# A last convolution by seven quarter products, group-norm sums on another engine, key products by chunk

## The chip, the core and the metric

The kernel runs on one core of a Trainium2 chip. The core has five engines with a queue each: TensorE (PE) multiplies matrices into PSUM, VectorE (DVE) and ScalarE (ACT) work elementwise and reduce, GpSimd (POOL) does a few elementwise operations, SyncE (SP) issues nearly all DMAs. Each engine works through its own instructions in order and waits on semaphores for the others. The metric is the time in microseconds of one execution; less is better.

## The reference

The input is 8 images of 512 channels of 32 x 32, in float32. Each goes through two layers with a residual each, `x = x + layer(group_norm(x))`, with group norms of 32 groups of 16 channels.

```
layer one:
  t  = silu(bn(conv1x1(gn(x), 512 -> 512)));  ys = [t[:256], t[256:]]
  twice (modules l = 0, 1):
      z = silu(bn(conv3x3(ys[-1], 256 -> 256)))
      q, k, v = conv1x1(z);  a = softmax(q . (k + rw + rh) / 8)   4 heads of 64
      ys.append(ys[-1] + silu(bn(conv1x1(a . v))))
  x = x + silu(bn(conv1x1(concat(ys), 1024 -> 512)))          the last convolution, "cv2"
layer two:
  h = relu(bn(depthwise3x3(gn(x))));  h = 0 where the channel's max |h| < 4
  h = relu(bn(conv1x1(h, 512 -> 512)));  h = 0 where the channel's max |h| < 0.001
  x = x + h
```

## The kernel before, in words

One loop over the 8 images (`for b in range(B)`, L958) issues all instructions. A small wrapper (`InOrder`, L33) keeps PE, DVE, ACT and SP in exactly the order in which the Python code issues them; the profile therefore shows L43 for nearly every instruction, and groups are told apart by tile names. Work of neighbouring images is interleaved by hand: lists of small pieces (`taps`, `stats`, `early`, `late`, `before`, `halves`, `finishes`) are emptied piece by piece with `pump(list, n)` between other work. So a piece's place in the code is its place in the engine queues.

An image passes these stages:

- cv1 (L520), the first 1x1 convolution, on 128 x 128 blocks of weights and 512 columns of the image: output chunks m = 2, 3 (tiles `ps_cv`, written to `yp[0]`) and then 0, 1 in halves (`ps_y`, to `y0`).
- conv3 (L559), the 3x3 convolution in a transformed domain: DVE makes six planes from `yp` in `vtmp`, `v` and the buffers `kr`, `vt`, `qy`, TensorE multiplies them (`ps_c`), DVE transforms back (`mid`, `sd`, `y`), ACT writes `z` by Silu.
- qkv (L707): key products for chunks 2 and 3 of the weights into two PSUM tiles `ps_qk`, each evicted by DVE into `kr` with the column term `rw` added (L736) and then given the row term by POOL (L737); value products `ps_v`, which reuse the same PSUM tiles; query products. Pieces of the list `bg` are pumped between them in the numbers `counts`.
- attention (L758): 32 steps of scores (`ps_s`), exponential on ACT (`e`), products with the values two steps later (`ps_av`), and a running sum of the exponentials on DVE (`sum`). At step 19 and after the last step, the sums over partitions are formed on TensorE (`ps_dn`), inverted on DVE and spread by two DMAs; z is scaled by them. Other work is pumped in at the steps in `QUIET` (L956). After the last step, `tail` issues TensorE work that covers the last inversion.
- cv2m (L880), the 1x1 convolution after the attention (`ps_m`), with its residual on DVE into `yp[1]` or `qy`.
- After the second module, cv2 (L898): for each of four output chunks m, eight input blocks k (`y0`, `yp[0]`, `yp[1]`, `qy`, two chunks each) times two halves n of 512 columns, 64 matmuls into a two-bank PSUM tile `ps_cv2`; ACT applies Silu over 1024 columns, DVE adds to `xt`. The weights come as four tiles of 512 KB in a ring of four SBUF buffers (`ring_sources`, L303), which also carries the other weights. A released buffer is refilled by the next DMA of the list.
- Layer two's front (L400): `group_norm` on `xt` in two groups of two chunks. For each chunk DVE makes `bn_stats` and `bn_aggr` (L366), then a small matmul with `g_sb` averages over the group (`pm`), DVE forms the deviations, a second small matmul (`pv`), POOL takes the power -1/2, ACT normalises into `xn` and multiplies by the middle tap into `ht`. Eight `taps` per chunk follow on DVE, Relu on ACT, and `prune` (L428): DVE's maximum, a comparison, and POOL's product with it. These taps lie in the cv2 stage and in the next image's cv1, qkv(0) and first attention.
- Layer two's back (L454): products `ps_pw`, in the next image's first module.

The last image has no successor; its layer two follows at once (L1089 to L1159), chunk by chunk. There `prune` uses `reaches` (L345), ACT's masked sum with a DVE comparison, and scales `wpw_sb` instead of `ht`. Image 0 has a cv2 of its own order, with parts of it begun beside its attention (`partial`), and it prepares the transformed weights of conv3.

PSUM has two two-bank tiles (`big`, for ps_s, ps_qk, ps_v, ps_c, ps_cv2), three single banks (`acc`, for ps_av, ps_m2, ps_y0, ps_pw) and one bank `mm` (pm, pv, ps_dn). SBUF has a pool of 11 work tiles of 128 x 1024.

Of the kernel before, what the change touches and what calls it, by code (L numbers as in the profile page):

```python
# [10 lines left out]
F32 = mybir.dt.float32  # L11
# [4 lines left out]
P = 128  # L16
# [47 lines left out]
def fast_kernel(  # L64
# [53 lines left out]
    def load(dst, b):  # L118
# [24 lines left out]
    u_dram = [  # L143
        [dram.tile([P, 2, 4, 2, P], F32, tag=f"u{l}_{i}", name=f"u{l}") for i in range(6)]
        for l in range(2)
    ]

    raw = [[t.rearrange("p a b -> p (a b)")[:, : 6 * C2] for t in (qy, kr, vt)]]
# [55 lines left out]
    def flat(ps):  # L204
        return ps.rearrange("p n f -> p (n f)")
# [5 lines left out]
    def phases(ap):  # L211

        return ap.rearrange("p (r h t) -> p r h t", h=F, t=F // 4)
# [10 lines left out]
    def pump(bg, n=1):  # L224

        for _ in range(min(n, len(bg))):
            piece = bg.pop(0)
            if piece is None:
                return
            piece()  # L230
# [72 lines left out]
    def ring_sources():  # L303
        for b in range(B):
            for l in range(2):
                for i in range(6):
                    yield u_dram[l][i].rearrange("p a b c d -> p (a b c d)"), 2048
                yield wqkv[:, l].rearrange("p k o -> p (k o)"), 1536
                if b == l == 0:
                    for m in range(2):  # L310
                        yield w2[:, :, m * P : (m + 1) * P], 1024
            for m in range(KC):
                yield w2[:, :, m * P : (m + 1) * P], 1024

# [32 lines left out]
    def reaches(t, i):  # L347


        keep = small.tile([P, 1], F32, tag="keep3", name="keep3")  # L350
        nc.scalar.activation(
            work_tile("over"), t, AF.Relu, bias=below[:, i : i + 1], accum_out=keep
        )
        nc.vector.tensor_scalar(keep, keep, 0.0, None, ALU.is_gt)
        return keep

    def group_norm(src, dst, chunks):

# [41 lines left out]
    def layer1_front(groups):  # L400

        norm = {}

        def normed(c):
            norm[c] = work_tile("xn")
            return norm[c]

        gn = [group_norm(xt, normed, chunks) for chunks in groups]  # L410

        def before(c):
            size = len(groups[0])
            gn[c // size][size + 2 + c % size]()
            nc.scalar.mul(ht[c], norm[c], dw[:, c, 4:5])

        def tap(c, t):
            dst, src = img(ht[c]), img(norm[c])
            dy, dx = t // 3 - 1, t % 3 - 1
            o = dst[:, max(0, -dy) : F - max(0, dy), max(0, -dx) : F - max(0, dx)]  # L420
            i = src[:, max(0, dy) : F - max(0, -dy), max(0, dx) : F - max(0, -dx)]
            nc.vector.scalar_tensor_tensor(o, i, dw[:, c, t : t + 1], o, ALU.mult, ALU.add)

        def relu(c):
            norm.pop(c)
            act(ht[c], ht[c], AF.Relu, BN4 + c)

        def prune(c):  # L428
            keep = small.tile([P, 1], F32, tag="keep", name="keep")
            nc.vector.tensor_reduce(keep, ht[c], AX.X, ALU.max)  # L430
            nc.vector.tensor_scalar(keep, keep, 4.0, None, ALU.is_ge)
            nc.gpsimd.tensor_scalar(ht[c], ht[c], keep, 1.0, ALU.mult, ALU.mult)

        if len(groups) == KC:

            def prune(c):

                keep = reaches(ht[c], 0)
                w = wpw_sb[:, c, :]
                nc.vector.tensor_scalar(w, w, keep, None, ALU.mult)  # L440

            return [list(g) for g in gn], before, tap, relu, prune
        taps = []
        for c in range(KC):
            mine = [lambda c=c, t=t: tap(c, t) for t in range(9) if t != 4]
            if c:

                mine[2] = lambda c=c, t=mine[2]: (t(), relu(c - 1))
                mine[5] = lambda c=c, t=mine[5]: (t(), prune(c - 1))
            taps += mine  # L450
        taps += [lambda: relu(KC - 1), lambda: prune(KC - 1)]
        return gn[0][:4], gn[1][:4], [lambda c=c: before(c) for c in range(KC)], taps

# [253 lines left out]
    def qkv(l, bg, counts):  # L707
        counts = list(counts)
        with Weights() as wt:
            w = wt[:, : 6 * C2].rearrange("p (k o) -> p k o", k=2)  # L710

            def products(ms):

                tiles = [big_tile("ps_qk") for _ in ms]
                for k in range(2):
                    for m, ps in zip(ms, tiles):
                        for n in range(2):
                            nc.tensor.matmul(
                                ps[:, n, :],
                                w[:, k, m * P : (m + 1) * P],  # L720
                                z[:, k, n * 512 : (n + 1) * 512],
                                start=(k == 0),
                                stop=(k == 1),
                            )
                return tiles

            pump(bg, counts.pop(0))
            for m, ps in enumerate(products((2, 3))):
                kk = phases(kr[:, m, :])
                full = [P, 4, F, F // 4]  # L730
                col = rw[:, l, m, :].rearrange("p (t r) -> p r t", r=4)
                row = rh[:, l, m, :].unsqueeze(1).unsqueeze(3)

                col = col.unsqueeze(2).to_broadcast(full)
                for r in (slice(0, 2), slice(2, 4)):
                    nc.vector.tensor_tensor(kk[:, r], phases(flat(ps))[:, r], col[:, r], ALU.add)  # L736
                nc.gpsimd.tensor_tensor(kk, kk, row.to_broadcast(full), ALU.add)  # L737
                pump(bg, counts.pop(0))
            for g in range(2):
                ps = ps_big.tile([P, 4, C2], F32, tag="big", name="ps_v")  # L740
                for j in range(4):
                    jt = 4 * g + j
                    for k in range(2):
                        nc.tensor.matmul(
                            ps[:, j, :],
                            z[:, k, jt * P : (jt + 1) * P],
                            w[:, k, 2 * C2 : 3 * C2],
                            start=(k == 0),
                            stop=(k == 1),
                        )  # L750
                nc.scalar.copy(vt[:, 4 * g : 4 * g + 4, :], ps)
                pump(bg, counts.pop(0))
            for m in range(2):
                (ps,) = products((m,))
                nc.scalar.copy(qy[:, m, :], flat(ps))
                pump(bg, counts.pop(0))
# [123 lines left out]
    def cv2m(l):  # L880
        for n in range(2):
            for m in range(2):
                ps = bank_tile("ps_m2")
                for k in range(2):
                    nc.tensor.matmul(
                        ps,
                        wm2_sb[:, l, k, m * P : (m + 1) * P],
                        z[:, k, n * 512 : (n + 1) * 512],
                        start=(k == 0),
                        stop=(k == 1),  # L890
                    )
                t = work_tile("m2")[:, :512]
                act(t, ps, AF.Silu, BN3 + 2 * l + m)
                r = slice(2 * n, 2 * n + 2)
                dst = inner(yp[1], m) if l == 0 else phases(qy[:, m, :])
                nc.vector.tensor_tensor(dst[:, r], phases(t), inner(yp[l], m)[:, r], ALU.add)

    def cv2():  # L898
# [53 lines left out]

        return products, finish, partial


    QUIET = (5, 8, 11, 14, 17, 18, 24, 26, 27, 28, 29, 30)  # L956
    halves, finishes, taps, before, late = [], [], [], [], []
    for b in range(B):  # L958
        if b:
# [1 line left out]
            pump(first)  # L961
            pump(taps, 2)
            pump(first)
            pump(taps, 2)
            pump(first)
            pump(late)
            pump(taps, 2)
            pump(first)
            pump(late)
            pump(taps)  # L970
            pump(before, 2)
            pump(y0_work, 2)
            conv3(0, y0_work, 1, [])
            if b + 1 < B:
# [55 lines left out]
        load(xt, b)  # L1030
        stats = group_norm(pt, lambda c: pt[c], range(KC)) if b + 1 < B else []
        qkv(1, [], (0,) * 7)
        if b:
            products, finish, _ = cv2()

        def beside():
            products(0, range(6) if b else (4, 5))
            if b == 0:
                products(1, (3, 4, 5))

        attention(stats[:KC], (6, 10, 14, 17), beside)
        stats = stats[KC:]
        cv2m(1)
        if b == B - 1:
            break
        early, late, before, taps = layer1_front(((0, 1), (2, 3)))
        if b:
            products(1, (0, 1, 2, 3))
        pump(stats)
        if b:  # L1050
            products(1, (4, 5))
        products(0, (6, 7))
        pump(stats)
        finish(0)
# [45 lines left out]
    pump(gn[0])  # L1100
    products(1, (2, 3, 4))
    pump(gn[0])
    products(1, (5,))
    pump(gn[0])
    before(0)
    products(1, (6, 7))
    taps(1)
    finish(1)
    pump(gn[1])
# [505 lines left out]
```

## Time and profile before

| | us |
|---|---|
| median of 4 runs (2679.45 to 2680.41) | 2680.34 |
| the profiled execution, as timed | 2679.96 |
| its span, from the first to the last instruction | 2678.2 |
| granted TensorE clock, mean over the span | 0.997 |
| one middle image, from cv2 to cv2 | 327.4 |
| DVE busy in one middle image | 239 |
| ACT busy in one middle image | 140 |

The page counts the busy time of each engine, follows the chain of work that ended last, and lists the costliest groups of instructions. A float32 matmul leaves two records in the profile. The windows give the busy time of each engine in a stretch of the span, and the timeline lists instructions in order of time with the idle time before them in brackets and what ended it. The middle images repeat each other to within 0.3 us.

### The profile page before, as it was taken

The numbers are of one execution on the slowest core, as the hardware profiler recorded it, in microseconds if no ns is written. First come the engines' busy times: TensorE is split into PE (matmuls) and PEld (weight loads), VectorE is DVE, ScalarE is ACT, GpSimd is POOL, SyncE is SP. The second block draws the span as 40 slices with busy tenths as digits, with TensorE's granted clock in tenths as the row PEclk, the third lists the DMA queues.
The fourth block names the chain that finished last, engine by engine and source line by source line (L and its number), as shares of the span: only waits on it lengthen the run. The fifth ranks groups of instructions, "written<-read, shape, count | busy, mean of one in ns | idle before, by whom it ended". The sixth has DMA issues, their size and how long they took to land.

```text
span 2678.2 us, 36189 instructions
## 1 busy us (share of the span) xinstructions
PE 2627.2 (98%) x14958; PEld 1414.2 (53%) x14958; DVE 1955.9 (73%) x2692; ACT 1152.5 (43%) x1417; POOL 162.5 (6%) x99
## 2 busy tenths in 40 slices
PE   7999999999999999999999999999999999999997
PEld 5364464644646446464465545655455654646443
DVE  8886598774986759766697667976578865888557
ACT  3535436252352534535345343444335343353533
POOL 1000010000100001000010000100001000010000
PEclk9999999999999999999999999999999999999998
DMA  8441231302303013030130302312122221303100
GB/s 329 150 151 43 71 130 32 130 20 69 138 25 130 17 63 138 25 130 17 63 138 27 128 17 78 123 60 95 32 91 95 75 79 48 106 32 99 56 16 33
DMA packets 89340, 220.78 MB, mean 82 GB/s; under 512 B 5840, under 2 KB 53200, under 8 KB 76624
## 3 DMA queue, kind: packets, MB, share of 16 engines
q1 hardware_dynamic: 85616, 214.98, 23.5%
q10 hardware_dynamic: 3552, 3.41, 0.4%
q8 instruction: 119, 1.95, 0.3%
q14 instruction: 53, 0.43, 0.1%
HBM read 172.23 MB, written 29.36 MB: 75 GB/s over the span
## 4 chain that ended last, share of the span: by engine, by line
PE 90%; DVE 5%; ACT 1%; DMA 1%; issue 1%; POOL 0%; SPq 0%; POOLq 0%; ACTq 0%; DVEq 0%
PE ps_cv L43 19%; PE ps_av L43 16%; PE ps_s L43 16%; PE ps_c L43 11%; PE ps_pw L43 7%; PE ps_qk L43 7%; PE ps_v L43 4%; PE ps_m L43 4%; PE ps_y L43 4%; DVE kr L43 1%; PE ps_dn L43 1%; DVE ht L43 1%; ACT qy L43 1%; DMA u<-ucomp 1%; DVE mid L43 0%
## 5 line engine op out<-in xcount | busy, mean ns | idle before, releaser
L43 ACT ACTIVATE e<-ps_s 128x1024 f32<-128x1024 f32 x512 | 524.2, 1024 | 281.0 <-PE ps_s L43 271.5
L43 PE MATMUL ps_s<-qy,kr 64*64 64x512 f32 x4096 | 571.7, 592 | 1.7 <-ACT e L43 0.2
L43 PE MATMUL ps_av<-e,vt 64*64 64x512 f32 x4096 | 570.9, 591 | 1.6 <-ACT part L43 1.6
L43 DVE TENSOR_TENSOR sum<-sum,e 128x1024 f32<-128x1024 f32 x384 | 471.3, 1227 | 83.1 <-ACT e L43 76.9
L43 DVE SCALAR_TENSOR_TENSOR ht<-xn,v_sb,ht 128x961 f32<-128x961 f32 (+1 forms) x256 | 336.0, 1318 | 25.0 <-ACT ht L43 19.9
L43 PEld LDWEIGHTS ps_av<-e,vt 64*64 64x64 f32 x4096 | 219.3, 133 | 232.2 <-issue 155.6
L43 PEld LDWEIGHTS ps_s<-qy,kr 64*64 64x64 f32 x4096 | 203.8, 133 | 250.8 <-issue 139.7
L43 PE MATMUL ps_pw<-ht,wpw_sb 128*128 128x512 f32 x512 | 226.7, 598 | 7.2 <-DVE wpw_sb L43 7.1
L43 PE MATMUL ps_cv<-yp,wring 128*128 128x512 f32 x512 | 231.0, 599 | 0.0
L43 PE MATMUL ps_qk<-z,wring 128*128 128x512 f32 x512 | 225.7, 593 | 3.3 <-ACT z L43 3.3
L43 DVE TENSOR_TENSOR sum<-e 128x1024 f32<-128x1024 f32 x64 | 78.4, 1224 | 174.7 <-ACT e L43 173.7
L43 PEld LDWEIGHTS ps_pw<-ht,wpw_sb 128*128 128x128 f32 x512 | 96.4, 191 | 129.7 <-issue 120.3
L43 PEld LDWEIGHTS ps_qk<-z,wring 128*128 128x128 f32 x512 | 96.8, 190 | 119.2 <-issue 110.8
L43 PEld LDWEIGHTS ps_cv<-yp,wring 128*128 128x128 f32 x512 | 96.4, 191 | 115.2 <-issue 114.4
L737 POOL TENSOR_TENSOR kr<-kr,v_sb 128x1024 f32<-128x1024 f32 x32 | 69.7, 2186 | 1042.1 <-DVE kr L43 1042.1
L43 ACT COPY c<-ps_c 128x256 f32<-128x256 f32 x96 | 35.5, 369 | 208.6 <-PE ps_c L43 202.4
L43 PE MATMUL ps_v<-wring,z 128*128 128x256 f32 x512 | 114.3, 381 | 8.2 <-DVE kr L43 8.2
L43 PEld LDWEIGHTS ps_c<-kr,wring 128*128 128x128 f32 x1024 | 116.8, 192 | 10.4 <-issue 6.0
L43 DVE RECIPROCAL r<-ps_dn 128x128 f32<-128x128 f32 x128 | 114.7, 927 | 6.9 <-ACT r L43 6.9
L43 PE MATMUL ps_c<-kr,wring 128*128 128x128 f32 x1024 | 117.3, 275 | 2.3 <-ACT kr L43 2.3
L43 PE MATMUL ps_c<-vt,wring 128*128 128x128 f32 x1024 | 117.3, 275 | 1.6 <-DMA wring<-u 0.9
L43 PE MATMUL ps_c<-qy,wring 128*128 128x128 f32 x1024 | 117.7, 276 | 0.2 <-issue 0.2
(138 smaller groups left out, 2982.4 us busy)
## 6 DMA issues: line engine op xcount, KB each, us to landing
wring<-u SPq DMA_DIRECT2D x96, 1024.0 KB, 4.8
wring<-in_w SPq DMA_DIRECT2D x34, 512.0 KB, 4.3
pt<-in_x SPq DMA_DIRECT2D x32, 512.0 KB, 5.9
rw<-r SPq DMA_DIRECT2D x64, 256.0 KB, 3.4
xt<-in_x SPq DMA_DIRECT2D x32, 512.0 KB, 6.0
out<-xt SPq DMA_DIRECT2D x32, 512.0 KB, 2.9
wring<-in_wqkv SPq DMA_DIRECT2D x16, 768.0 KB, 4.3
u<-ucomp SPq DMA_DIRECT2D x24, 256.0 KB, 3.4
```

The source lines that it names most:

```text
L43: made = method(*args, **kwargs)
L737: nc.gpsimd.tensor_tensor(kk, kk, row.to_broadcast(full), ALU.add)
```

## The change

Three things change, and the schedule of the pumped pieces with them.

1. For images 1 to 6, cv2 is computed by seven products of quarters (Strassen's scheme in Winograd's form): weights and inputs are seen as 2 x 2 blocks (256 outputs by 512 inputs, 512 inputs by 512 columns). Four combinations of the weights, s1 to s4, and copies of a11, a12 and a22 are made once in image 0, during its second attention, and stored in DRAM; the ring brings them as two tiles of 1536 and two of 2048 columns instead of four of 1024. Four combinations of the inputs, t1 to t4, are made by DVE in every such image (in `kr`, `z`, `vt` and two work tiles), and the outputs are put together from the products by DVE additions. Silu then works on halves of 512 columns. Images 0 and 7 keep the eight products.
2. Layer two's group norm, in all images, takes its sums on ACT: a Copy with accumulated output, then, after the mean, a Square with the mean as bias and accumulated output. In images 0 to 6 `prune` of chunks 0 and 1 uses `reaches` in place of DVE's maximum.
3. The key products of qkv run chunk by chunk instead of input block by input block (except in image 0), and the two half additions of the column term become one.

```diff
+    QUARTERS = (("a11", "s1", "a12"), ("s2", "s3", "a22", "s4"))
+    s_dram = [ [ dram.tile([P, len(q), 4, P], F32, ...) for i, q in enumerate(QUARTERS) ] for p in range(2) ]
...
+            if 0 < b < B - 1:
+                for i in range(2):
+                    for p in range(2):
+                        yield s_dram[p][i].rearrange("p q k o -> p (q k o)"), 512 * (3 + i)
+                continue
             for m in range(KC):
                 yield w2[:, :, m * P : (m + 1) * P], 1024
...
+    def group_norm_scalar(src, dst, chunks):
...
+        def over(i, c, func, o, **bias):
+            nc.scalar.activation(ht[c], src[c], func, accum_out=o[:, i : i + 1], **bias)
+        def means():
+            nc.tensor.matmul(pm[:, :n], g_sb, sums, start=True, stop=True)
+            nc.vector.tensor_scalar(gm, pm[:, :n], -1.0 / HW, None, ALU.mult)
+            for i, c in enumerate(chunks):
+                over(i, c, AF.Square, sq, bias=gm[:, i : i + 1])
+        def deviations():
+            nc.tensor.matmul(pv[:, :n], g_sb, sq, start=True, stop=True)
+            nc.vector.tensor_scalar(rs, pv[:, :n], 1.0 / HW, 1e-5, ALU.mult, ALU.add)
+            nc.gpsimd.tensor_tensor(rs, rs, mhalf[:, :n], ALU.pow)
...
+        work = [lambda i=i, c=c: over(i, c, AF.Copy, sums) for i, c in enumerate(chunks)]
...
-        gn = [group_norm(xt, normed, chunks) for chunks in groups]
+        gn = [group_norm_scalar(xt, normed, chunks) for chunks in groups]
...
         def prune(c):
+            if c < 2:
+                keep = reaches(ht[c], 0)
+            else:
                 keep = small.tile([P, 1], F32, tag="keep", name="keep")
                 nc.vector.tensor_reduce(keep, ht[c], AX.X, ALU.max)
...
-                for k in range(2):
-                    for m, ps in zip(ms, tiles):
+                order = [(k, i) for i in range(len(ms)) for k in range(2)]
+                for k, i in sorted(order) if by_input else order:
...
-            for m, ps in enumerate(products((2, 3))):
+            for m, ps in enumerate(products((2, 3), b == 0)):
...
-                for r in (slice(0, 2), slice(2, 4)):
-                    nc.vector.tensor_tensor(kk[:, r], phases(flat(ps))[:, r], col[:, r], ALU.add)
+                nc.vector.tensor_tensor(
+                    kk, phases(flat(ps)), col.unsqueeze(2).to_broadcast(full), ALU.add
+                )
...
+    def combine_weights(p):
+...
+    def quartered():
+        rights = {
+            "a11": b11, "s1": t1, "a12": b21, "s2": t2, "s3": t3, "a22": t4, "s4": b22,
+        }
+        def product(p, name, cs=range(4)):
...
+                nc.tensor.matmul(
+                    banks[p, name],
+                    w[:, QUARTERS[i].index(name), c, :],
+                    rights[name][c],
+                    start=(c == 0),
+                    stop=(c == 3),
+                )
...
+        def keep_first():
...
+                nc.scalar.copy(kept[p, "m1"], banks[p, "a11"])
...
+        def plus(p, o, x, name):
...
+            nc.vector.tensor_tensor(kept[p, o], kept[p, x], banks[p, name], ALU.add)
...
+        def finish(p, low, n, x, name):
...
+            nc.vector.tensor_tensor(t, kept[p, x], banks[p, name], ALU.add)
+            act(t, t, AF.Silu, BN1 + m)
...
             pump(first)
             pump(taps, 2)
             pump(first)
-            pump(taps, 2)
-            pump(first)
             pump(late)
             pump(taps, 2)
             pump(first)
             pump(late)
-            pump(taps)
-            pump(before, 2)
+            pump(taps, min(3, len(taps) - 19))
+            pump(before)
+            pump(first)
+            pump(taps, min(2, len(taps) - 18))
+            pump(before)
             pump(y0_work, 2)
...
+            def beside():
+                for p in range(2):
+                    product(p, "a11")
+                keep_first()
+                right(0, range(4))
+                for p in range(2):
+                    product(p, "a12", (0, 1))
...
+        attention(work, (2, 4, 6, 8, 10, 11, 12, 14, 16, 18) if b == 0 else (6, 10, 14, 17), beside)
...
         if b:
-            products(1, (0, 1, 2, 3))
+            right(1, (0, 1))
+            product(0, "s1")
+            right(1, (2, 3))
+            product(0, "a12", (2, 3))
+            product(1, "a12", (2, 3))
+            finish(0, 0, 0, "m1", "a12")
+            right(2, (2, 3))
+            finish(1, 0, 0, "m1", "a12")
+            settle()
+            pump(stats)
+            product(0, "s2")
+            plus(0, "u2", "m1", "s2")
+            plus(0, "u4", "u2", "s1")
+            less4(range(4))
+            pump(stats)
+            product(0, "s3")
+            pump(stats, 2)
+            plus(0, "u3", "u2", "s3")
+            finish(0, 1, 1, "u4", "s3")
+            product(0, "a22")
+            pump(stats, 2)
+            finish(0, 1, 0, "u3", "a22")
+            settle()
+            product(0, "s4")
+            finish(0, 0, 1, "u4", "s4")
...
+            halves, finishes = layer1_back(b)
+            continue
...
-    products(1, (5,))
+    products(1, (5, 6))
     pump(gn[0])
     before(0)
-    products(1, (6, 7))
+    products(1, (7,))
```

`combine_weights` forms s1 = a21 + a22, s2 = s1 - a11, s3 = a11 - a21 and s4 = a12 - s2. `right` and `less4` form t1 = b12 - b11, t2 = b22 - t1, t3 = b22 - b12 and t4 = b21 - t2. `settle` adds the finished halves to `xt` on DVE. The products of the second 128 rows of each block (p = 1), left out above, follow in the same way, with the pieces of `early`, `before` and `late` and 4 taps between them.

For images 1 to 6, 4 taps lie beside the products and 9 in the next image's cv1, where there were 9 and 7; the rest go to qkv(0), 12 pieces, and the first attention.

## The prediction

> **What bounds the kernel now.** I read the page first, then the windows of one middle image (image 3 becoming image 4), then that stretch's timelines of each engine.
>
> ```profile
> PE 2627.2 (98%) x14958; PEld 1414.2 (53%) x14958; DVE 1955.9 (73%) x2692; ACT 1152.5 (43%) x1417; POOL 162.5 (6%) x99
> ...
> PE 90%; DVE 5%; ACT 1%; DMA 1%; issue 1%; POOL 0%; SPq 0%; POOLq 0%; ACTq 0%; DVEq 0%
> ```
>
> TensorE is busy 98% of the span and carries the chain: a matmul taken away is worth its whole time, provided that no other engine makes TensorE wait afterwards. The windows say where that could happen (columns: window, its length, then busy time and count of PE, PEld, DVE, ACT, POOL, the granted clock, DMA share, GB/s).
>
> ```profile
> 1251.00:1327.00 76.00, 76.00 (x192) 34.22 (x185) 37.54 (x57) 22.51 (x24) 1.72 (x2) 1.00 0.19 62
> 1327.00:1371.00 44.00, 43.59 (x246) 31.04 (x244) 40.31 (x75) 16.70 (x26) 3.52 (x2) 1.00 0.51 186
> 1385.00:1443.00 58.00, 57.88 (x529) 27.08 (x528) 50.26 (x49) 38.04 (x42) 3.90 (x2) 1.00 0.09 29
> ```
>
> The first window is the last convolution and cv1: DVE is half idle. The second, conv3 and the key products, and the third, the first attention, leave DVE 3.7 and 7.7 us: DVE work pushed there has little cover. The key products show how close it is already:
>
> ```profile
> 1360.13 3.60 PE L43 MATMUL ps_y<-pt,w_sb 128*128 128x512 f32 x8
> 1363.56 7.03 PE L43 MATMUL ps_qk<-z,wring 128*128 128x512 f32 x16
> 1371.09 7.14 PE L43 MATMUL ps_v<-wring,z 128*128 128x256 f32 x32 [0.50 <-DVE kr L43]
> ```
>
> TensorE waits for the eviction `kr`, because the value products need its PSUM tile. On DVE:
>
> ```profile
> 1364.02 3.75 DVE L43 SCALAR_TENSOR_TENSOR ht<-xn,v_sb,ht 128x961 f32<-128x961 f32 x3
> 1368.91 3.97 DVE L43 TENSOR_TENSOR kr<-ps_qk,v_sb 128x512 f32<-128x512 f32 x4 [1.14 <-PE ps_qk L43]
> ```
>
> Three taps fill the time until the keys come. ACT at that moment changes its table:
>
> ```profile
> 1365.28 0.76 ACT L43 ACTIVATE y<-ps_y,bi,sc 128x512 f32<-128x512 f32 x1
> 1366.05 1.28 ACT L43 ACT_TABLE_LOAD   x1
> 1367.34 0.20 ACT L43 ACTIVATE warm<-warm 128x1 f32<-128x1 f32 x1
> ```
>
> At the end of the first attention the softmax sums are just in time: DVE's last `sum` starts at 1440.95 and takes 1.22, the TensorE product `ps_dn` that reads it starts at 1442.23, having been free from 1442.0.
>
> **The change, part by part.** All against the profiled execution: 2679.96 us, of which 2678.2 span; the median shown is 2680.34, 0.4 above it.
>
> *Fewer products.* Images 1 to 6 do 7 x 8 = 56 matmuls of 512 columns where they did 64. A run of 16 records (two per matmul) takes 6.87 in the chain, so a matmul is 0.859; the operand rows (`yp`, `qy`, `y`) agree within 2 ns, so slices and combinations should run alike. Eight are 6.87 per image, **-41.2** in six. The clock was 1.00 in all windows, so nothing comes from there.
>
> *What the scheme adds.* Per image 16 subtractions of 128x512 (0.61 apart, as `vtmp`), 6 partial sums and 8 additions from PSUM (0.60, as `z<-ps_av`), 8 half-size additions to `xt`, 0.69, for four of 1.22; ACT gets two copies (0.58) and eight half Silus (0.67 apart) for four of 1.20. Off DVE go 4 x 1.5 of statistics, the small steps and two reductions of 1.21. I laid both queues beside TensorE from 1251.4 in their program order. The first combination lies under the reciprocals and their DMA, ready at 1258.2; t2 ends at 1272.8, its product starts at 1275.7; t4's first chunk 1281.0, product 1282.7; each PSUM bank is free 1 us or more before its next product; the norm's mean product comes 1.5 after its sums. All hidden there. The four ring tiles carry 28 blocks in place of 16 of cv2's weights (1.5 MB more per image); the last is freed at 1307 and the weights loaded behind it are wanted 35 us later. Only the second norm product waits: its squares on ACT come after cv1's Silu, 0.2 late, in seven images: **+1.4**. TensorE reaches conv3 6.9 earlier and DVE 7 earlier (13 taps before it, where there were 16), so conv3 stays as tight as it was.
>
> *Keys by chunk.* The first key tile is ready after 4 matmuls, not 6, 1.72 earlier, and the 0.65 wait before `ps_v` goes (1371.09 less 1363.56 + 6.87) in the second module of images 1 to 7 and the first of image 1: **-5.2**. Joining two 512-column additions changes little (3.97 for four).
>
> *First module of images 2 to 7.* Three taps fewer are done earlier, so the first item pumped here now ends in `reaches(ht[0])`: ACT's masked sum, and DVE's comparison waits for it, with two taps and both `kr` queued behind. ACT is behind its Silu, table load and `warm`: 1367.45, + 1.14 + 0.19 (row `over`) = 1368.8. Then two taps of 1.25 = 1371.3, slowed by the POOL product that starts with them: six taps beside such a product took 8.19 against 7.42 without, +0.8, so 1372.1; `kr` 1.98, so `ps_v` starts near 1374.1. DVE enters conv3 some 0.4 earlier than before, so I take 1373.8: 2.7 later than before. Bounds: -0.65 (no wait left) and +3.9 (DVE stands still for POOL's whole 1.95). **+16.2** in six. [...]
>
> *First attention of images 2 to 7.* Seven taps lie in it instead of four, and the reductions of chunks 2 and 3 move from steps 8 and 18 to 17 and 27. From step 17 (1415.4) to the last sum I count on DVE 14 sums of 1.13 (15.8), 4 `z` of 0.60 (2.4), 4 reciprocals of 0.87 (3.5), 3 taps of 1.22 (3.7), 2 reductions with comparison of 1.32 (2.6), end latency 0.1: 28.1, nearly without a gap, so 1443.5, plus up to 0.8 for each of two POOL products. I take 1444.6 against 1442.2: **+14.4** in six, 2.4 each; bounds 0 (DVE catches up) and 5.2 (DVE stands still for both POOL products of 1.95: 1447.4). ACT's last Relu now waits for the tap at step 24 and holds up an exponential; that delay lies inside this one.
>
> *Tail.* Per chunk 1.5 and three steps of 0.2 leave DVE; ACT gets two passes of 1.33 each. The last two chunks' taps gain: `xn` of chunk 3 comes at 2637.7 instead of 2640.78, and the last comparison (2659.04) some 3.5 to 4 earlier. Against that, DVE waits for ACT's masked sum behind a square. Bounds 0 and -6.3 (all that leaves DVE for chunks 1 to 3); **-3.5**.
>
> *Image 0.* Eight weight sums (0.61, some 4.9) and two 1 MB loads lie in its second attention, where DVE has over 10 us free; 14 stores on SP precede only that attention's spreads. Taken as 0; if the loads come late, DVE waits, at most the 4.8 that a 1 MB load takes to land.
>
> Sum: -41.2 - 5.2 - 3.5 + 1.4 + 16.2 + 14.4 = -17.9; 2679.96 - 17.9 = **2662**.
>
> **The rivals.**
> - *The two new waits are not there* (DVE catches up, the masked sum comes early). For: before, both places cost 0.7 or less. Against: queue order fixes who stands behind whom. Without the second: 2662 - 14.4 = 2648. Without the first, and `ps_v`'s 0.65 gone too in six: 2662 - 16.2 - 3.9 = 2642. Without both: 2628.
> - *They are larger* (DVE standing still for each POOL product): 1.2 and 2.8 more per image, 24 in six, 2686 at worst; a part of it, 2668 to 2675. For: the reductions and taps there run back to back. Against: the 8.19 of six taps.
> - *Slower: DVE comes late to conv3.* TensorE's first product there had 2.5 us to spare (`kr`'s first component at 1336.2, the product at 1338.7). If the chains product, partial sum, Silu, `xt`, taps run 2.5 + 3.0 = 5.5 us later than I laid them, six images cost 18 and the gain is gone; at 8 us late, 2695. Against: DVE is idle half of that window.
> - *The change does not do what it says* would need slower matmuls; the rows of all operands are alike.
>
> **How the numbers follow.** The sum as forecast, 2652 to 2668: 0.50. One wait absent, 2642 to 2648: 0.18. Both absent, about 2628: 0.08. Larger waits, 2668 to 2675: 0.10. About even (within 0.2%, which is 5.4 us and about what a measurement can tell): 0.04. Slower by conv3: 0.10. So faster 0.86, same 0.04, slower 0.10. The range 2637 to 2676 leaves out both absent and the slower case.
>
> **What would show it.** In the changed profile: `ps_cv` with 96 records fewer, and 6.9 us less of it per middle image; `ps_v` behind `kr` about 3 us in first modules of images 2 to 7 and none in second modules; `keep3` on DVE waiting for ACT `over`; `ps_dn` waiting 2 to 3 us for DVE `sum`, once per image from 2 on; `pv` waiting 0.2 for ACT; no wait of the quarter products. A TensorE wait at `ps_c` for `kr` or `yp`, or at a quarter product for DVE, would make the prediction wrong on the slow side; taps that end early enough to leave `ps_dn` alone, on the fast side.

## The result, and the profile after

The changed kernel took 2684.44 us (median of 40 runs, 2679.8 to 2688.61) against 2679.85 for the kernel before, measured beside it (60 runs): a ratio of 1.0016, 95% interval 1.0012 to 1.0021. It is a hair slower, where 2662 was forecast. The profiled execution took 2685.99 us, 2684.1 of it span; against the profiled execution of before that is +6.0, where the sum said -17.9. So 23.9 us have to be found.

The page after, its line of busy times and its chain of work that ended last:

```profile
PE 2604.7 (97%) x14862; PEld 1364.6 (51%) x14862; DVE 2000.1 (75%) x2708; ACT 1251.7 (47%) x1609; POOL 162.8 (6%) x99
...
PE 76%; DVE 16%; ACT 4%; issue 2%; DMA 1%; POOL 0%; ACTq 0%; SPq 0%; POOLq 0%; DVEq 0%
```

TensorE is busy 22.5 us less, and 96 records of matmuls are gone, as the change says. But DVE had 5% of the chain and now has 16%, and ACT went from 1% to 4%: TensorE waits for them where it did not before. The list of what TensorE waited for in the changed kernel says where (total us, times, longest):

```profile
PE ps_v L43 <- DVE kr L43: 19.6, 8, 3.1
PE pv L43 <- DVE d L43: 8.7, 8, 1.2
PE ps_dn L43 <- DVE sum L43: 8.2, 6, 1.4
```

The windows of the same image as before, image 3 becoming image 4, cut at stage boundaries (length, then busy time and count of PE, PEld, DVE, ACT, POOL, granted clock, DMA share, GB/s):

```profile
1250.60:1332.70 82.10, 80.94 (x201) 36.33 (x199) 55.11 (x84) 40.93 (x54) 3.25 (x3) 1.00 0.17 58
1332.70:1367.80 35.10, 32.02 (x217) 25.59 (x215) 29.57 (x58) 10.57 (x19) 1.97 (x1) 1.00 0.64 232
1367.80:1443.30 75.50, 73.90 (x577) 30.36 (x577) 67.20 (x60) 43.08 (x48) 10.82 (x5) 1.00 0.07 22
1443.30:1578.20 134.90, 134.82 (x867) 75.86 (x865) 96.57 (x136) 58.75 (x77) 3.94 (x2) 1.00 0.26 88
```

In the first three TensorE is no longer busy all the time: 1.2, 3.1 and 1.6 us idle. From the starts in TensorE's timelines, for this image (us; the last two columns are two of the experiments below, the one with eight products again and the fastest one, with all five corrections):

| stretch, from the first product of one to that of the next | before | after | after - before | forecast | eight products | all corrected |
|---|---|---|---|---|---|---|
| last convolution and cv1 (`ps_cv` to `ps_c`) | 87.28 | 82.01 | -5.27 | -6.67 | 87.44 | 80.58 |
| conv3 and keys (`ps_c` to `ps_v`) | 32.40 | 35.25 | +2.85 | +2.7 | 31.99 | 31.98 |
| rest of the first module (`ps_v` to `ps_pw`) | 72.13 | 75.43 | +3.30 | +2.4 | 72.01 | 72.01 |
| second module (`ps_pw` to the next `ps_cv`) | 135.58 | 134.87 | -0.71 | -0.65 | 134.86 | 134.85 |
| whole image | 327.39 | 327.56 | +0.17 | -2.2 | 326.30 | 319.42 |

The keys, as TensorE, DVE and ACT have them in their timelines:

```profile
1357.43 7.28 PE L43 MATMUL ps_qk<-z,wring 128*128 128x512 f32 x16
1367.81 7.17 PE L43 MATMUL ps_v<-wring,z 128*128 128x256 f32 x32 [3.09 <-DVE kr L43]
```
```profile
1357.89 1.21 DVE L43 SCALAR_TENSOR_TENSOR ht<-xn,v_sb,ht 128x961 f32<-128x961 f32 x1
1362.58 0.15 DVE L43 TENSOR_SCALAR keep<-keep 128x1 f32<-128x1 f32 x1 [3.48 <-ACT over L43]
1362.65 3.23 DVE L43 SCALAR_TENSOR_TENSOR ht<-xn,v_sb,ht 128x992 f32<-128x992 f32 x2
1365.80 3.86 DVE L43 TENSOR_TENSOR kr<-ps_qk,v_sb 128x1024 f32<-128x1024 f32 x2
```
```profile
1359.91 1.28 ACT L43 ACT_TABLE_LOAD   x1
1361.21 0.20 ACT L43 ACTIVATE warm<-warm 128x1 f32<-128x1 f32 x1
1361.32 1.13 ACT L43 ACTIVATE over<-ht,below 128x1024 f32<-128x1024 f32 x1
```

This is the forecast's queue, item by item: `over` behind the table load, DVE's comparison 3.48 us idle for it, two taps and `kr` behind the comparison, and TensorE 3.09 idle for `kr`. The two taps beside POOL's product took 3.23; the two of 1.25 that were forecast and the 0.8 for POOL make 3.3.

The wait that the forecast did not have is in the first stretch, the next image's norm:

```profile
1274.83 3.68 PE L43 MATMUL ps_cv2q<-z,wring 128*128 128x512 f32 x8
1279.67 0.39 PE L43 MATMUL pv<-d,g_sb 128*128 128x4 f32 x2 [1.17 <-DVE d L43]
```
```profile
1276.70 0.68 DVE L43 TENSOR_TENSOR c<-part,ps_cv 128x512 f32<-128x512 f32 x1
1277.29 0.70 DVE L43 TENSOR_TENSOR xt<-c,xt 128x512 f32<-128x512 f32 x1
1278.26 0.70 DVE L43 TENSOR_TENSOR xt<-c,xt 128x512 f32<-128x512 f32 x1 [0.27 <-ACT c L43]
1278.87 0.15 DVE L43 COPY gm<-pm 128x4 f32<-128x4 f32 x1
...
1279.45 0.16 DVE L43 TENSOR_TENSOR d<-d,mv 128x4 f32<-128x4 f32 x1
```

`pm` was done at 1275; DVE reads it at 1278.87, after the two additions to `xt`, the second of which waits for a Silu. `d` comes at 1279.5, `pv` could have run at 1278.3.

And the clock. Ten microseconds from `ps_v` on, in images 4 and 6 (windows; the granted clock is the third number from the end):

```profile
1367.80:1377.80 10.00, 9.99 (x39) 7.52 (x40) 9.82 (x7) 3.16 (x4) 4.82 (x2) 1.00 0.00 0
...
2022.90:2032.90 10.00, 9.96 (x33) 8.26 (x34) 9.82 (x7) 1.01 (x1) 4.80 (x2) 0.71 0.00 0
```

The same wait of 3.09 us stands ahead of both. Behind the second, and behind that of image 7 (0.84), the clock is halved for 6.83 and 3.41 us (0.50 in the windows from 2021.92 and from 2353.01), and these two images take 330.4 and 329.1 us instead of 327.55: 4.4 us. Why these two and not the other four is worked out in the last section.

The 23.9 us, then: the norm's wait 6 x 1.4 = 8.4, the attention 6 x 0.9 = 5.4, the tail 5.5 (-3.5 forecast, +2.0 measured), the clock 4.4, the keys 6 x 0.15 = 0.9; together 24.6, against which the second modules stand with -0.4; that is 24.2, within 0.3 of the difference.

### The profile page after: what moved, and what is told of

The parts are those of the page before. It is cut to its first block, busy times and chain, and to the rows that moved or that the text cites. A ratio compares the mean times of both kernels' runs of the same rounds, so it can differ in the third digit from the quotient of the medians.

```text
span 2684.1 us, 36237 instructions
## 1 busy us (share of the span) xinstructions
PE 2604.7 (97%) x14862; PEld 1364.6 (51%) x14862; DVE 2000.1 (75%) x2708; ACT 1251.7 (47%) x1609; POOL 162.8 (6%) x99
## 3 DMA queue, kind: packets, MB, share of 16 engines
q1 hardware_dynamic: 70512, 230.19, 24.6%
q10 hardware_dynamic: 3552, 3.41, 0.4%
q8 instruction: 119, 1.95, 0.3%
## 4 chain that ended last, share of the span: by engine, by line
PE 76%; DVE 16%; ACT 4%; issue 2%; DMA 1%; POOL 0%; ACTq 0%; SPq 0%; POOLq 0%; DVEq 0%
PE ps_s L43 13%; PE ps_av L43 13%; PE ps_cv L43 9%; PE ps_pw L43 7%; PE ps_c L43 7%; PE ps_cv2q L43 7%; PE ps_qk L43 6%; PE ps_v L43 4%; DVE sum L43 4%; PE ps_m L43 4%; PE ps_y L43 3%; DVE mid L43 2%; DVE ht L43 2%; DVE y L43 1%; PE ps_dn L43 1%
## 5 line engine op out<-in xcount | busy, mean ns | idle before, releaser
L43 PE MATMUL ps_s<-qy,kr 64*64 64x512 f32 x4096 | 583.6, 593 | 2.9 <-ACT e L43 0.7
L43 PE MATMUL ps_av<-e,vt 64*64 64x512 f32 x4096 | 584.1, 591 | 1.4 <-ACT part L43 1.4
L43 PEld LDWEIGHTS ps_av<-e,vt 64*64 64x64 f32 x4096 | 206.1, 133 | 254.0 <-issue 198.5
L43 PEld LDWEIGHTS ps_s<-qy,kr 64*64 64x64 f32 x4096 | 191.1, 133 | 269.7 <-issue 164.8
L43 PEld LDWEIGHTS ps_v<-wring,z 128*128 128x128 f32 x512 | 99.7, 196 | 43.8 <-DVE kr L43 26.2
L43 PE MATMUL ps_cv<-pt,w_sb 128*128 128x512 f32 x256 | 116.6, 606 | 0.0
L43 PEld LDWEIGHTS ps_c<-qy,wring 128*128 128x128 f32 x1024 | 116.1, 192 | 0.4 <-issue 0.3
```

The source lines that it names most:

```text
L43: made = method(*args, **kwargs)
```

## The experiments

Two theories. *Separate waits*: each of these losses has its own cause, in who stands behind whom in DVE's queue, and goes when that order is mended. *DVE is full*: it has too much to do in all, and a wait taken away comes back in the next place. All ratios are to the kernel before, beside which each was timed (2678.9 to 2679.3 us).

**The comparison later.** The masked sum stays where it is on ACT; what reads it moves behind a later tap.

```diff
             if c < 2:
-                keep = reaches(ht[c], 0)
+                keep = masked[c] = small.tile([P, 1], F32, tag="keep3", name="keep3")
+                nc.scalar.activation(
+                    work_tile("over"), ht[c], AF.Relu, bias=below[:, :1], accum_out=keep
+                )
+                return
...
+        def cut(c):
+            keep = masked.pop(c)
+            nc.vector.tensor_scalar(keep, keep, 0.0, None, ALU.is_gt)
             nc.gpsimd.tensor_scalar(ht[c], ht[c], keep, 1.0, ALU.mult, ALU.mult)
...
+            if c > 1:
+                mine[0] = lambda c=c, t=mine[0]: (t(), cut(c - 2))
```

> Edit: the comparison (and the product on GpSimd behind it) of the pruning of chunks 0 and 1 is put behind the first tap two chunks later; ScalarE's masked sum stays where it is, so only VectorE's wait for it goes. Theory W (separate waits): the 3.09 us that TensorE waits for kr in the first module of images 2 to 7 goes to 0 to 0.3 (18 us in six images), and with it the half clock seen after two of these waits (some 4 us): 2661 to 2664 us. Theory T (VectorE has too much work as a whole, so that a wait taken away only moves): the time comes back at the softmax sums or at conv3, 2678 us or more.

2661.36 us, 0.9938 (0.9925 to 0.9952). DVE in the same place:

```profile
1352.17 3.76 DVE L43 SCALAR_TENSOR_TENSOR ht<-xn,v_sb,ht 128x961 f32<-128x961 f32 x3
1355.84 2.05 DVE L43 TENSOR_TENSOR kr<-ps_qk,v_sb 128x1024 f32<-128x1024 f32 x1
1359.04 1.99 DVE L43 TENSOR_TENSOR kr<-ps_qk,v_sb 128x1024 f32<-128x1024 f32 x1 [1.15 <-PE ps_qk L43]
```

Three taps without a pause, and DVE then waits for TensorE. The wait before `ps_v` is gone, no clock is halved in the middle images, and nothing came back: `ps_dn` waits 8.2 as before. One comparison of 0.15 us in the wrong place cost 23 us, the waits and the clock behind two of them.

**The norm's mean first.**

```diff
             finish(1, 0, 0, "m1", "a12")
-            settle()
             pump(stats)
+            settle()
```

> Edit: the mean step of the next image's norm is put ahead of the first two additions to xt on VectorE. Theory W: the 1.2 to 1.4 us that TensorE waits for d in images 1 to 6 go: 7 to 8 us less than the changed kernel's 2684.4, about 2676.5. Theory T: the time comes back in the same image at ps_v or ps_dn: 2683 to 2685.

2683.65 us, 1.0017 (1.0008 to 1.0026): no gain. By the times that is the second theory. The stages say otherwise: `ps_cv` to `ps_c` did shrink, to 80.58, 1.43 less, and no wait in the middle images is longer. But `ps_v` to `ps_dn` took 49.4 to 49.5 in all six images, 1.6 more, and the windows show why (ten microseconds from `ps_v`, images 2, 4 and 6):

```profile
713.00:723.00 10.00, 9.92 (x35) 7.96 (x36) 9.82 (x8) 2.04 (x3) 4.81 (x2) 0.83 0.00 0
...
1368.60:1378.60 10.00, 10.00 (x36) 8.02 (x37) 9.82 (x7) 2.15 (x3) 4.81 (x2) 0.83 0.00 0
...
2024.00:2034.00 10.00, 9.97 (x36) 8.00 (x37) 9.82 (x7) 2.16 (x3) 4.80 (x2) 0.83 0.00 0
```

The clock is halved after every one of the six waits of 3.09, where it was after two. So neither theory as stated; a third: *the clock takes the gain back*. (The waits are as long as before; what changed is where they lie in the grid of the clock's changes, as the last section shows.)

**Both together**, to test that.

> Edit: both the late comparison and the norm's mean step first. In the run with the mean step first alone the 1.4 us came off the stretch before conv3 in every image, but the granted clock then halved behind all six waits of ps_v, 3.4 us each, and gave the gain back. Theory C (the clock takes it back, since the wait of 3.09 us falls in a bad place of the clock's window): with no wait of 3 us left in the middle images, the mean step is worth its full 1.4 x 6 = 8.5: 2661.4 - 8.5, 2652 to 2654 us. Theory T (VectorE's work only moves): nothing again, 2660 to 2662.

2651.37 us, 0.9893 (0.9878 to 0.9909): 10 less than with the late comparison alone. Once no wait of 3 us is left, the mean step is worth what it is worth, and the clock is 1.00 in all six windows.

**A longer wait.** One more copy on ACT ahead of `over`.

```diff
             if c < 2:
+                if c == 0:
+                    nc.scalar.copy(work_tile("twice"), ht[c])
                 keep = reaches(ht[c], 0)
```

> Edit: one more copy of 1024 columns on ScalarE (about 1.05 us) ahead of the masked sum of chunk 0, so that VectorE and with it TensorE's wait at ps_v last that much longer, 4.1 to 4.2 us in images 2 to 7. If it is the length of the wait that halves the clock behind it, all six now pay 1.7 to 3.4 us of clock where the changed kernel had two: 6.5 for the waits and 6 to 12 for the clock, 2697 to 2703. If the clock has another cause: 6.5 alone, 2691.

2701.21 us, 1.0081 (1.0067 to 1.0095). The wait is 4.03 or 4.04 us, all six windows behind it are at 0.83 to 0.73, and `ps_v` to `ps_dn` takes 49.5 to 50.4:

```profile
1376.38 9.72 PE L43 MATMUL ps_v<-wring,z 128*128 128x256 f32 x32 [4.04 <-DVE kr L43]
```

Here it is the wait that halves the clock: six times 0.95 us more of wait cost 16.8 us, about 10 of them by the clock.

**The taps of the attention earlier.**

```diff
-    QUIET = (5, 8, 11, 14, 17, 18, 24, 26, 27, 28, 29, 30)
+    QUIET = (3, 5, 7, 9, 11, 13, 15, 17, 26, 28, 29, 30)
```

> Edit: the seven taps left for the first attention are issued at steps 3, 5, 7, 9, 11, 13, 15 in place of 5, 8, 11, 14, 17, 18, 24; the last Relu at 17, the last reduction at 26 as before. Theory W: VectorE is no longer behind at the last softmax sum; the wait of ps_dn (2.0 us, 2.6 with two small ones before it) shrinks to 0 to 0.8: 9 to 15 us less, 2669 to 2675. Theory T: VectorE is full in the whole attention, so earlier taps make the earlier sums late, tiles of e come free later and the exponentials wait: 2682 or more.

2668.99 us, 0.9967 (0.9955 to 0.9979). `ps_v` to `ps_pw` is 72.9 where the clock holds, 2.5 less. DVE was not full in the attention; the steps at which the taps were issued put them just ahead of the sums that TensorE wants last.

**The tail's statistics on DVE.**

```diff
-        gn = [group_norm_scalar(xt, normed, chunks) for chunks in groups]
+        kind = group_norm if len(groups) == KC else group_norm_scalar
+        gn = [kind(xt, normed, chunks) for chunks in groups]
...
-    products(1, (5, 6))
+    products(1, (5,))
...
-    products(1, (7,))
+    products(1, (6, 7))
```

> Edit: in the last image alone the statistics of layer two go back to VectorE, with the order of the last convolution there as before. The two traces' tails differ by 2.0 us (118.9 against 116.9 from the last convolution's first product on), so by them 2682.4. By the forecast's term (the tail gains 3.5 from ScalarE) it would be 2688.

2681.54 us, 1.0015 (1.0006 to 1.0024): by the times not to be told from the changed kernel. The traces say more: from the last image's first `ps_cv` to the end, the six kernels with statistics on DVE took 114.1 to 117.0, mean 115.7, and the eight with sums on ACT 116.0 to 119.0, mean 118.2. The half clock in this stretch is the same on the mean (17.5 and 17.4 us of it). So the tail loses some 2.5 by ACT's sums and the order that goes with them, from single executions whose ranges overlap a little; it does not gain 3.5.

**All four together.**

> Edit: late comparison, mean step first, early taps, and the last image's statistics on VectorE, together. If the four are separate waits, the gains add: 2684.4 - 23.1 - 8.5 - 15.4 - 2 = 2635 us, up to 2640. If they share a cause, or if early taps are already caught up by the late comparison, one of the terms is missing: 2645 to 2653.

2636.03 us, 0.9834 (0.9821 to 0.9848). The gains add: the losses were separate.

**And the last reduction earlier**, step 19 in place of 26.

> Edit: the four corrections together as before, and the last reduction of chunk 3 at step 19 of the first attention in place of 26, so that it stands ahead of the reciprocals and not ahead of the last sums. In the corrected kernel ps_dn to ps_pw still takes 25.38 us against 24.60 without a wait. If the reduction just ahead of the last sums makes this 0.78, six images give 4.7 back: 2631 to 2632 us. If VectorE is simply full from there on, nothing or a loss: 2636 to 2640.

2630.85 us, 0.9816 (0.9803 to 0.983), as worked out: the last 0.78 per image was one reduction ahead of the last sums. This is the fastest of all, 1.8% under the kernel before; DVE is as busy as in the changed kernel, 2000.6 us, and has 4% of the chain:

```profile
PE 2587.5 (98%) x14862; PEld 1395.9 (53%) x14862; DVE 2000.6 (76%) x2732; ACT 1241.2 (47%) x1593; POOL 157.4 (6%) x99
...
PE 92%; DVE 4%; ACT 1%; DMA 1%; issue 1%; POOL 0%; SPq 0%; ACTq 0%; POOLq 0%; DVEq 0%
```

**Eight products again**, the rest of the change kept: in images 1 to 6 the last convolution and its order are those of before, and the weight combinations are out.

```diff
-            if 0 < b < B - 1:
-                for i in range(2):
-                    for p in range(2):
-                        yield s_dram[p][i].rearrange("p q k o -> p (q k o)"), 512 * (3 + i)
-                continue
...
-        if 0 < b < B - 1:
+        if False:
             product, keep_first, plus, finish, settle, right, less4 = quartered()
```

> Edit: the seven quarter products out, the last convolution of images 1 to 6 again by eight products with the order that image 0 has, the weight combinations out; ScalarE's norm sums, the pruning by ScalarE and the key products by chunk stay. By the forecast's term TensorE gets 41.2 us more, and the norm's wait for d (8.5) goes: 2684.4 + 41.2 - 8.5 = 2717 us. Rival (what the scheme saves on TensorE was hidden, another engine sets the time): 2690 to 2700.

2672.96 us, 0.9976 (0.9967 to 0.9985). Both expected times were wrong, 2717 and 2690 to 2700: it is 11 *less* than with seven products. TensorE's list of waits has no `ps_dn`, and of `ps_v`

```profile
PE ps_v L43 <- DVE kr L43: 1.1, 2, 0.7
```

is all. Without the scheme three more taps are done ahead of conv3, `over` with them, and the two waits do not arise. Against the fastest kernel, which has no such wait either, an image takes 326.30 to 319.42: 6.88, the eight matmuls to a hundredth (6.87). In the changed kernel the stretches with the three waits took 1.43 + 3.27 + 3.42 = 8.1 back, more than the products saved.

**The three taps ahead of conv3 in the changed kernel too.**

```diff
-            pump(taps, min(3, len(taps) - 19))
+            pump(taps, min(5, len(taps) - 19))
             pump(before)
             pump(first)
-            pump(taps, min(2, len(taps) - 18))
+            pump(taps, min(3, len(taps) - 18))
```

> Edit: in the changed kernel, three more taps ahead of conv3, so that 18 pieces are left behind it in images 2 to 7, as the kernel before and the version with eight products have, and not 21. Theory P (the two waits come from where these three taps lie): the waits at ps_v (3.1) and ps_dn (3) go with their half clock, and VectorE comes 2.5 to 4 us later to conv3, of which 1.1 is spare: 1.4 to 2.9 at ps_c. 2684.4 - 4.4 - 18.5 - 18 + 8 to 17: 2652 to 2661 us. Theory L (VectorE is late as a whole, the place does not matter): what goes at ps_v and ps_dn comes at ps_c and in conv3, 2675 or more.

2683.24 us, 1.0014 (1.0005 to 1.0023). The waits at `ps_v` and `ps_dn` went, and one came at conv3 instead; DVE, then TensorE:

```profile
1326.30 1.22 DVE L43 SCALAR_TENSOR_TENSOR ht<-xn,v_sb,ht 128x961 f32<-128x961 f32 x1
1331.05 0.15 DVE L43 TENSOR_SCALAR keep<-keep 128x1 f32<-128x1 f32 x1 [3.53 <-ACT over L43]
1331.12 3.23 DVE L43 SCALAR_TENSOR_TENSOR ht<-xn,v_sb,ht 128x992 f32<-128x992 f32 x2
```
```profile
1337.71 7.50 PE L43 MATMUL ps_c<-kr,wring 128*128 128x128 f32 x43 [4.05 <-issue]
```

The comparison waits for `over` here as well, 3.53 us, now ahead of conv3's first combinations, and the clock is halved with all six waits, which are 4.05 long (0.73 and 0.74 in the ten microseconds from `ps_c`). Theory P failed, since the comparison moved with the taps; but DVE is not full either: it stands idle for those 3.53 us. (TensorE's wait has no releaser in the profile; that it is for `kr`'s component is read from DVE's times, 1336.92 to 1339.3.)

**The other two parts, each undone for the most part in the kernel with the four corrections (2636.03 us).** Key products by input everywhere, `products((2, 3), True)`; the joined addition of the column term stays:

> Edit: the corrected kernel with the key products by input again in all modules (the third part of the change undone alone). By the forecast's term: 0.65 before ps_v in the second modules of seven images and 0 to 0.65 in the first modules of six: 2636 + 4.6 to 2636 + 8.5, 2640.6 to 2644.5 us. Rival (the order of the four products makes no difference, joined evictions make it up): 2636.

2642.97 us, 0.9861 (0.9846 to 0.9876), 7 more: 0.5 before `ps_v` in second modules, 0.3 in first ones, and 0.1 in each from there to `ps_dn`; 0.96 per image, 6.7 in seven. Layer two's statistics on DVE in all images, `kind = group_norm`; the pruning by `reaches` stays:

> Edit: the corrected kernel with layer two's norm statistics on VectorE in all images (the second part of the change undone alone; the last image has it so already). VectorE gets 4 x 1.5 us more and ScalarE 8 passes of 1.1 to 1.3 less, in a stretch where VectorE idles a third. If that idle time holds it: 2634 to 2638 us, so that moving the sums to ScalarE buys nothing. If the taps and conv3 come up to 6 us later: a wait at ps_c of 1 to 5 us in six images, 2642 to 2666.

2649.64 us, 0.9889 (0.9874 to 0.9904), 13.6 more. `ps_cv` to `ps_c` is 81.47 (+0.9) and `ps_c` to `ps_v` 33.48 (+1.5). That is 2.36 per image. So the sums on ACT are worth 13.6 ahead of the last image, and cost some 2.5 in the last.

## Why the prediction was wrong

The direction was wrong. Both large waits that it named were there, where it put them; what failed is the sum around them. A wait in the next image's norm was taken as hidden (8.4 us), the clock behind the forecast's own wait of 3 us was put at nothing (4.4), the attention's wait was sized too small (5.4), and the tail had the wrong sign (5.5). Step by step:

- *Fewer products, -41.2:* right; 6.88 per image between two kernels without waits.
- *"The clock was 1.00 in all windows, so nothing comes from there":* wrong. TensorE's longest wait in that stretch was 0.50; the forecast itself put one of 3 us in, and behind two of its six the clock was halved. It cost 4.4 in the profiled execution. The times of the changed kernel go with it: mean clock 0.997 at 2679.8 to 2681.2 us, 0.994 at 2685.9 to 2688.6.
- *"All hidden there", the scheme's DVE work beside the products:* the products are indeed never late, but the queue was followed for them and for layer two's norm, not for the next image's norm, whose `d` stands behind `settle`. +1.4 was allowed in all for the second norm product; the stretch lost 1.6 per image, 8.4 more than forecast.
- *Keys by chunk, -5.2:* right: `ps_v` follows `ps_qk` without a gap in second modules, and `ps_pw` to `ps_v` there went from 63.45 to 62.80, the 0.65. Undone, it costs 7, since without the 3 us wait the first modules have a part in it too.
- *First module, +16.2:* right, 2.85 per image against 2.7. The row of six taps beside POOL's product gave 0.8, and that held: two taps took 3.23 beside it. But the forecast set that row against a DVE that stands still for POOL's whole 1.95, and that price was too high. Those 1.95 us are POOL's product beside a busy DVE, and it is slowed there itself: with the comparison later it meets an idle DVE once in each of six images and takes 1.12. A loss of 0.7 to 0.8 therefore does not show that DVE goes on beside it.
- *First attention, +14.4:* the place was right, the size 3.3 and not 2.4. DVE reached the counted stretch 0.3 later (`ps_v` to `ps_dn` 47.83, where before it was 47.54), and each of POOL's two products cost it about 0.8, where 1.1 was taken for both:

```profile
1417.73 2.10 DVE L43 SCALAR_TENSOR_TENSOR ht<-xn,v_sb,ht 128x992 f32<-128x992 f32 x1
1435.46 3.27 DVE L43 TENSOR_TENSOR sum<-sum,e 128x1024 f32<-128x1024 f32 x2
```

  A tap without POOL takes 1.25 and two sums 2.54. From 1412.41, the first of the 14 sums, to the end of the last at 1442.21 DVE took 29.8: the 28.1 counted and 1.6 for POOL.
- *"Off DVE go 4 x 1.5 of statistics":* taken as hidden, without a term of its own. Undone in the kernel with the four corrections it costs 13.6, since conv3 and the key products start later.
- *Tail, -3.5:* the sign was wrong. DVE lost its 1.5 per chunk, but TensorE's `pm` now waits for a Copy on ACT, which waits for `xt`, and DVE's `gm` for that:

```profile
2636.89 1.06 ACT L43 ACTIVATE ht<-xt 128x1024 f32<-128x1024 f32 x1 [0.76 <-DVE xt L43]
2637.86 0.19 ACT L43 ACTIVATION_READ_ACCUMULATOR ht<-xt 128x1 f32 x1
2637.95 1.13 ACT L43 ACTIVATE over<-ht,below 128x1024 f32<-128x1024 f32 x1
...
2640.04 1.15 ACT L43 ACTIVATE ht<-xt,gm 128x1024 f32<-128x1024 f32 x1 [0.87 <-DVE gm L43]
```

  `over` stands between the two passes and DVE's comparison ahead of `gm`, so `xn` of the last chunk is applied at 2645.60, 80.5 after that image's first `ps_cv`, where before it was 79.6. That is 0.9 of the tail's 2.0; where the other 1.1 behind it comes from was not followed.

The rival that came nearest was "they are larger", with 2686 at worst, but by luck: POOL's products cost DVE 0.7 to 0.8 each and not 1.95, and most of what was missing lay in the norm, the clock and the tail. "The two new waits are not there" is what the fastest kernel makes true, and its price was nearly right: 2628 then, 2630.85 measured.

## What to carry to other kernels

A change that takes work off the bounding engine moves every fixed order of the others against it: follow each queue once for every value that the bounding engine waits for, the small norms included, and ask of each instruction that waits for another engine what stands behind it. A comparison of 0.15 us, in the queue ahead of work that TensorE waited for, cost 23 us here, and all of it came back by moving it. Where two versions of the order are possible, compare stages by their starts and not by the total, since a loss elsewhere can hide a real gain.

## What the hardware showed

In the middle images of these traces a wait of TensorE of 3.09 us stands in four kernels, six times in each, and one of 4.04 in two. Behind the 3.09 the granted clock halved after two of six in the changed kernel, two of six with the early taps, two of six with the tail's statistics on DVE, and all six with the mean step first; with the 4.04 it halved all twelve times. The other waits there, 1.37 us at the longest in the changed kernel, did not.

Which of them do can be read from where they lie. In each trace's record of the granted clock all changes lie on a grid of 3.413 us (3.4133 in the changed kernel's), to 0.005 us, and in the middle images each half-clock stretch is one or two steps of it, 3.41 or 6.83 us long. Laid on that grid, most of the 36 waits fall into two steps. In the 12 that cost no clock the larger part, within one step, is 1.57 to 1.99 us; in the 24 that did it is 2.07 to 3.10, and the half clock begins with the next step. Where 1.02 us or more of the wait lay in that next step, the step after it was at half clock too; at 0.33 or less it was not. In the changed kernel the larger parts are 1.58, 1.72, 1.85, 1.96, 2.07 and 2.76, in order: an image of 327.56 is a little less than 96 steps, so the same wait moves along the grid, and the last two are those that cost clock. With the mean step first they are 2.96 to 3.10, nearly the whole wait. In the first and last images, where several short waits share a step, the border is less sharp: 1.77 us idle in a step was enough once, 2.02 was not another time. In the changed kernel's trace, from 18.3 us on, where the record begins, half clock set in there behind steps with 2.39 to 3.03 us idle and not behind those with 1.94 or less.

With the mean step first the images take 327.7 or 327.8 us, with the three taps ahead of conv3 327.6 to 327.9, and 96 steps are 327.68; with the longer wait, from image 3 on, they take 331.0 to 331.1, and 97 steps are 331.09. That an image locks on to a whole number of steps, so that a small gain is lost until the wait itself goes, fits these three periods, but no run here separates it from chance.
